# Macaron block on Trainium2: the l part of an item's queries as VectorE's first work in its place of a step

## The chip, the cores and the metric

The kernel runs on one core of a Trainium2 chip, in one launch. The metric is the device time of an execution in microseconds (us).

The core has five engines that run side by side, each through its own list of instructions in order: TensorE (PE in the profile, with its weight loads as PEld), VectorE (DVE), ScalarE (ACT), GpSimd (POOL) and SyncE (SP), which here issues nearly all the DMA transfers. They wait for each other through semaphores. An engine whose next instruction has to wait holds up all that stands behind it in its list.

## The reference, cut to what matters

The input is 4 batches of 4096 rows with 512 columns. Three parts follow each other, each added to the rows:

```python
x = x + 0.5 * ffn(layernorm(x))          # quantised 512x512 product
x = x + attention(layernorm(x))          # 16 heads of 32, 13 neighbours
x = x + 0.5 * ffn(layernorm(x))
```

`ffn` quantises its input in blocks of 32 to a 6-bit grid with a scale per block, multiplies by a weight that is quantised the same way, and adds a bias. `attention` is neighbourhood attention:

```python
qkv = (x @ qkv_w.T + qkv_b).reshape(B, L, 3, HEADS, HEAD_DIM).transpose(2, 0, 3, 1, 4)
q, k, v = (qkv[0] * SCALE, qkv[1], qkv[2])
attn = jnp.einsum('bhld,bhlkd->bhlk', q, kg) + rpb[:, bidx][None]   # kg: 13 keys around each query
attn = jax.nn.softmax(attn, axis=-1)
out = jnp.einsum('bhlk,bhlkd->bhld', attn, vg)
return out.transpose(0, 2, 1, 3).reshape(B, L, C) @ proj_w.T + proj_b
```

## The kernel before

**Numbers in two halves.** Each float32 operand of a large product is held as two float16 parts, h (the value rounded to float16) and l (what the rounding left). `product` (L146) adds three of the four cross products: 12 matmuls of 128x512 into one bank of PSUM. ScalarE writes h, VectorE computes l from the exact value and h. For the queries and keys these are `put_high` (L367) and `put_low` (L371): both read the product in PSUM, and `put_low` reads the h part too.

**Tiles and items.** The rows are cut into 128 tiles of 128 rows. Four tiles make a group. Of each group the attention works on four items, one for each 128 columns (four heads), so there are 128 items as well. A tile goes through `first_half` (the first ffn and the second layernorm), `values`, `project_out` and `second_half`; an item goes through `project_qk`, `softmax` and `attend`. `quantised_norms` makes the quantised input of the two ffns, for two tiles together, and brings it into transposed form by a DMA into `xT`.

**The order is written by hand.** Time is cut into slots. A stage is a generator that ends a piece of work with `yield n, rank`, which puts its next piece n slots later at that rank. Within a slot the pieces run by rising rank:

```python
def run_slot(slot):
    for _, stage in sorted(slots.pop(slot, ()), key=lambda e: e[0]):
        for n, rank in stage:
            begin(slot + n, stage, rank)
            break
```

From L772 on the schedule is manual: each engine gets its instructions in the order in which the pieces run. A new tile and a new item start every 7 slots, so that one round of 7 slots repeats. By its number modulo 7, what each slot holds, in its order of ranks:

- slot 3: the product of an item's queries, `pmqk`; then the product of attention weights and values, `pv`
- slot 4: ScalarE copies `pv` to the ring (L530); VectorE makes the l parts `hlq` and `hln` (L204), and the DMAs that transpose them follow; the product of the item's keys, also `pmqk`; ScalarE writes the queries' h part (L369) and the halo (L382), and the exponentials `sf` (L469)
- slot 5: VectorE writes the l part of the ring (L536); ScalarE the normalised rows `yq` (L233); VectorE the softmax sums `total` (L472 to L474); TensorE the first ffn's product `pmf`; then the second piece of `project_qk`: VectorE the queries' l part (L373) and ScalarE the keys' h part (L369); GpSimd adds biases to two tiles `x` (L564)
- slot 6: VectorE the keys' l part (L373); block maxima `sc` and their reciprocals `r` (L239 to L244); TensorE the values' product `pmv`; GpSimd multiplies `sf` by `total` (L476)
- slot 0: GpSimd scales `yq` by `r` (L246); the second ffn's product `pmf`; scores `ps`
- slot 1: VectorE adds the table to the scores (L458 to L461) and adds the second ffn's product (L275); ScalarE makes the fp8 form `q` (L249) and the attention weights `p` (L480, L481)
- slot 2: the output projection `pmo`; GpSimd scales `q` back (L251)
- slot 3, later ranks: GpSimd makes the l part of `p` (L483), and a DMA transposes it to `pT` (L485)

Every second round some transfers `vs<-vd` (L409) that gather the values for later items are issued as well.

**PSUM.** The products `pmqk`, `pmf`, `pmv` and `pmo` share a pool of three banks, `ps_m` (L93), in the order in which they are begun. A round begins six: queries, keys, `pmf`, `pmv`, the second `pmf`, `pmo`. So `pmv` gets the bank that held the queries' product, and the second `pmf` the one that held the keys'.

Of the kernel before, what the change touches and what calls it, by code (L numbers as in the profile page):

```python
# [64 lines left out]
def macaron_kernel(  # L65
# [80 lines left out]
    def product(pm, lhs, rhs):  # L146

        n = 0
        for a, b in ((0, 1), (1, 0), (0, 0)):
            for c in range(KC):  # L150
                nc.tensor.matmul(  # L151
                    pm, lhs(a, c), rhs(b, c), start=(n == 0), stop=(n == 3 * KC - 1)
                )
                n += 1
# [189 lines left out]
    def item_of(m):  # L344

        g, c = divmod(m, KC)
        return g // NG, g % NG, c

    def project_qk(m):

        b, g, c = item_of(m)
        xg = x2[b * NG + g]
        t = qkp.tile([P, 2, 2, KN + GT], F16, tag="qk", name=f"qk{m}")
        qk[m] = t
        pms = []

        def project(s):
            pm = ps_m.tile([P, GT], F32, tag="mm", name=f"pmqk{s}_{m}")
            pms.append(pm)
            o = (QO, KO)[s] + c * P  # L360
            product(
                pm,
                lambda a, kc: wt[:, a, kc, o : o + P],
                lambda a, kc: xg[:, a, kc].rearrange("p i q -> p (i q)"),
            )

        def put_high(s):  # L367
            bias = qk_b[:, s, c : c + 1]
            nc.scalar.activation(t[:, s, 0, KN:], pms[s], AF.Identity, bias=bias)  # L369

        def put_low(s):  # L371
            bias = qk_b[:, s, c : c + 1]
            nc.vector.scalar_tensor_tensor(  # L373
                t[:, s, 1, KN:], pms[s], bias, t[:, s, 0, KN:], ALU.add, ALU.subtract
            )

        project(0)
        yield 1, 5
        project(1)
        put_high(0)  # L380
        if g > 0:
            nc.scalar.copy(t[:, :, :, :KN], halo[:, c])  # L382
        yield 1, 6
        put_low(0)
        put_high(1)
        if c == KC - 1:
            del x2[b * NG + g]
        yield 1, 0
        put_low(1)
        yield 2, 8  # L390
        if g + 1 < NG:
            nc.scalar.copy(halo[:, c], t[:, :, :, GT:])
# [217 lines left out]
    for m in range(n_items):  # L610
        k = m * STEP
        begin(k + QK, project_qk(m))
        begin(k + SC, softmax(m), 6)
        begin(k + PV, attend(m), 6)
# [297 lines left out]
```

## Time and profile before

| | us |
|---|---|
| median of 3 runs | 2442.0 |
| lowest and highest of them | 2439.76 and 2442.17 |
| the profiled execution's own time | 2436.42 |
| its span, from the first to the last instruction | 2434.6 |
| busy: PE, DVE, POOL, ACT | 2295.3, 2039.3, 1988.3, 1321.0 |

Steps below are worked out on the profiled execution. A line of the timeline gives the start in us from the start of the span, the duration in us, the engine, the line of the code, the operation, the tiles (out<-in), shapes and a count, and in brackets how long the engine sat idle before it and who ended that. Instructions of a kind that follow each other are merged; `x12` is a whole product. Records of matmuls overlap by a little, since their ends are modelled, so products are best compared by their starts.

### The profile page before, as it was taken

Reading aid. Unit: us, or ns where it says so; the run is one execution under the profiler, and the core shown is the slowest. Engines: PE = TensorE matmul, PEld = TensorE weight load, DVE = VectorE, ACT = ScalarE, POOL = GpSimd, SP = SyncE. Lnnn points to the kernel's source line nnn. Section 1 sums busy time; section 2 is a strip of 40 time slices with the busy share of each in tenths; the row PEclk is TensorE's granted clock in tenths of the full one; section 3 lists DMA queues with packets and bytes.
Section 4 is the critical chain, followed back from the end, with each engine's and each line's share of the span. In section 5 each row is a group of like instructions: output and inputs, shape, how many; then the busy total and the mean of one; then the engine's idle time right before and its main releaser. Section 6 shows DMA issues by size and latency. Waiting matters only on the chain.

```text
span 2434.6 us, 82394 instructions
## 1 busy us (share of the span) xinstructions
PE 2295.3 (94%) x35539; PEld 1113.3 (46%) x35539; DVE 2039.3 (84%) x3588; ACT 1321.0 (54%) x2080; POOL 1988.3 (82%) x2012
## 2 busy tenths in 40 slices
PE   0799999999999999999999999999999999999986
PEld 0344444444444444444444444444444444444442
DVE  8788888888888888888888888888888888888776
ACT  4455555555555555555555555555555555555442
POOL 5578888888888888878888888888888888888777
PEclk9899999999999999999999999999999999999998
DMA  5678788787787777778877778777777777777753
GB/s 154 143 145 153 153 161 156 143 152 150 147 159 155 148 147 157 147 144 157 154 146 158 144 152 157 155 148 152 154 140 154 156 157 139 159 148 143 135 110 92
DMA packets 925701, 360.59 MB, mean 148 GB/s; under 512 B 718876, under 2 KB 889752, under 8 KB 925336
## 3 DMA queue, kind: packets, MB, share of 16 engines
q1 hardware_dynamic: 924992, 354.79, 74.4%
q8 instruction: 278, 4.55, 0.8%
q14 instruction: 87, 0.71, 0.1%
q10 hardware_dynamic: 344, 0.53, 0.1%
HBM read 110.15 MB, written 67.29 MB: 73 GB/s over the span
## 4 chain that ended last, share of the span: by engine, by line
PE 67%; DVE 16%; ACT 8%; DMA 5%; issue 3%; POOL 2%; SPq 0%; ACTq 0%; POOLq 0%; DVEq 0%
PE pmf L151 16%; PE pmqk L151 16%; PE pmo L151 13%; PE pmv L151 12%; PE ps L433 6%; DVE total L474 4%; DMA xT<-hlq 4%; DVE total L472 3%; PE pv L503 3%; ACT sf L469 3%; ACT qk L369 2%; DVE qk L373 2%; ACT ring L530 1%; DVE total L473 1%; ACT qk L382 1%
## 5 line engine op out<-in xcount | busy, mean ns | idle before, releaser
L151 PE MATMUL pmf<-wt,xT 128*128 128x512 f16 x3048 | 702.7, 380 | 18.1 <-DMA xT<-hlq 17.7
L151 PE MATMUL pmqk<-x,wt 128*128 128x512 f16 x3072 | 708.6, 380 | 6.0 <-DMA x<-hln 5.3
L151 PEld LDWEIGHTS <-xT 128*128 128x128 f16 x3048 | 296.9, 98 | 386.6 <-DMA xT<-hlq 31.0
L151 PEld LDWEIGHTS <-wt 128*128 128x128 f16 x3072 | 290.2, 98 | 343.3 <-issue 10.2
L246 POOL TENSOR_TENSOR yq<-yq,r 128x1024 f32<-128x1024 f32 (+1 forms) x141 | 246.3, 1747 | 200.5 <-DVE r L244 200.5
L151 PE MATMUL pmv<-wt,x 128*128 128x512 f16 x1536 | 353.5, 380 | 23.5 <-DVE qk L373 14.4
L151 PE MATMUL pmo<-wt,ring 128*128 128x512 f16 x1536 | 356.2, 382 | 2.8 <-issue 2.5
L310 ACT CAST vt<-pmv 128x512 f16<-128x512 f32 x128 | 74.9, 585 | 469.1 <-PE pmv L151 469.1
L564 POOL TENSOR_TENSOR x<-x,half_ffn_b 128x512 f32<-128x512 f32 x256 | 327.3, 1279 | 0.1
L275 DVE SCALAR_TENSOR_TENSOR x<-pmf,coef,x 128x512 f32<-128x512 f32 x256 | 179.7, 702 | 136.9 <-PE pmf L151 136.5
L530 ACT ACTIVATE ring<-pv 128x510 f16<-128x510 f32 (+8 forms) x224 | 82.3, 414 | 368.4 <-PE pv L503 368.4
L180 DVE BATCH_NORM_STATS2 stn<-x 128x6 f32<-128x512 f32 x384 | 265.3, 691 | 9.3 <-DMA x<-in_L_attn_x_dram 0.6
L151 PEld LDWEIGHTS <-x 128*128 128x128 f16 x1536 | 149.9, 98 | 221.6 <-issue 46.4
L251 POOL TENSOR_TENSOR yq<-q,sc 128x1024 f32<-128x1024 fp8e4 (+1 forms) x141 | 246.6, 1749 | 0.0
L249 ACT ACTIVATE q<-yq,nudge 128x1024 fp8e4<-128x1024 f32 (+1 forms) x141 | 150.0, 1064 | 141.6 <-POOL yq L246 133.4
L151 PEld LDWEIGHTS <-ring 128*128 128x128 f16 x1536 | 140.5, 98 | 162.5 <-issue 5.5
L233 ACT ACTIVATE yq<-x,nbq,rsq 128x512 f32<-128x512 f32 x254 | 194.5, 809 | 31.4 <-POOL nbq L192 26.3
L476 POOL TENSOR_TENSOR sf<-sf,total 128x714 f32<-128x714 f32 (+2 forms) x128 | 178.6, 1395 | 37.9 <-DVE total L474 37.4
L483 POOL TENSOR_TENSOR p<-sf,p 128x714 f16<-128x714 f32 (+2 forms) x128 | 192.5, 1504 | 1.2 <-ACT p L480 1.1
L186 POOL TENSOR_SCALAR rsq<-mv 128x2 f32<-128x2 f32 (+1 forms) x141 | 132.0, 936 | 75.0 <-DVE mv L181 72.4
L467 POOL TENSOR_TENSOR sf<-sf,top 128x714 f32<-128x714 f32 (+2 forms) x128 | 180.3, 1409 | 13.8 <-DVE top L465 13.3
L458 DVE TENSOR_TENSOR sf<-ps,table 128x210 f32<-128x210 f32 (+5 forms) x288 | 126.4, 485 | 74.9 <-PE ps L433 74.4
(145 smaller groups left out, 3524.9 us busy)
## 6 DMA issues: line engine op xcount, KB each, us to landing
vs<-vd SPq DMA_DIRECT2D x144, 357.0 KB
x<-in_L_attn_x_dram SPq DMA_DIRECT2D x128, 256.0 KB
vd<-vt SPq DMA_DIRECT2D x128, 256.0 KB
out_dram<-x SPq DMA_DIRECT2D x128, 256.0 KB
vs<-vd SPq DMA_DIRECT2D x24, 378.0 KB
vs<-vd SPq DMA_DIRECT2D x24, 315.0 KB
rows<-in_L_attn_qkv_w_dram SPq DMA_DIRECT2D x12, 256.0 KB
xT<-hlq SPq DMA_TRANSPOSE x141
```

Of the source, the lines that this page charges most:

```text
L151: nc.tensor.matmul(pm, lhs(a, c), rhs(b, c), start=(n == 0), stop=(n == 3 * KC - 1))
L180: nc.vector.bn_stats(st, xs[t])
L233: nc.scalar.activation(y[:, u], xs[t], AF.Identity, bias=nb[:, u : u + 1], scale=rs[:, u : u + 1])
L246: nc.gpsimd.tensor_tensor(yb, yb, bc(r, QB), ALU.mult)
L249: nc.scalar.activation(q8, y, AF.Identity, bias=nudge, saturate=False)
L251: nc.gpsimd.tensor_tensor(yb, q8.rearrange("p u (n q) -> p (u n) q", q=QB), bc(sc, QB), ALU.mult)
L275: nc.vector.scalar_tensor_tensor(xs[t], pm, cf, xs[t], ALU.mult, ALU.add)
L433: nc.tensor.matmul(ps[rows, u, :sides, w * KN : (w + 1) * KN], t[rows, 0, part, q0 : q0 + QR], t[rows, 1, :sides, k0 : k0 + KN], start=par ...
L467: nc.gpsimd.tensor_tensor(s, s, bc(top[:, :n], KN), ALU.subtract)
L476: nc.gpsimd.tensor_tensor(s, s, bc(total[:, :n], KN), ALU.mult)
L483: nc.gpsimd.tensor_tensor(p[:, :n, KN : 2 * KN], s, ph, ALU.subtract)
L564: nc.gpsimd.tensor_tensor(xs[t], xs[t], b, ALU.add)
```

## The change

`project_qk` yields rank -1 in place of 6 ahead of its third piece. The piece holds `put_low(0)`, VectorE's l part of the queries, and `put_high(1)`, ScalarE's h part of the keys. It stays in the same slot (slot 5 modulo 7), where it ran after the rank 0 piece of the ring, the rank 1 piece of the norms, the rank 4 piece of the sums and the rank 5 product `pmf`, and now runs ahead of all of them. No instruction is added, removed or altered, and no DMA is in the piece.

```diff
         if g > 0:
             nc.scalar.copy(t[:, :, :, :KN], halo[:, c])
-        yield 1, 6
+        yield 1, -1
         put_low(0)
         put_high(1)
         if c == KC - 1:
```

## The prediction

> **What bounds the kernel now.** First the page: busy shares, and the row of the product that stands next after the moved piece.
>
> ```profile
> PE 2295.3 (94%) x35539; PEld 1113.3 (46%) x35539; DVE 2039.3 (84%) x3588; ACT 1321.0 (54%) x2080; POOL 1988.3 (82%) x2012
> ...
> L151 PE MATMUL pmv<-wt,x 128*128 128x512 f16 x1536 | 353.5, 380 | 23.5 <-DVE qk L373 14.4
> ```
>
> TensorE leads, and the idle time ahead of `pmv` names DVE's L373, a part of the queries or keys. The 14.4 us are a floor, since records of matmuls overlap and hide the first part of each gap. So next the timeline of PE, once in a round that waits and once in one that doesn't:
>
> ```profile
> 1354.17 2.76 PE L151 MATMUL pmqk<-x,wt 128*128 128x512 f16 x12
> 1356.77 2.75 PE L151 MATMUL pmf<-wt,xT 128*128 128x512 f16 x12
> 1359.70 2.75 PE L151 MATMUL pmv<-wt,x 128*128 128x512 f16 x12 [0.18 <-DVE qk L373]
> 1362.68 2.76 PE L151 MATMUL pmf<-wt,xT 128*128 128x512 f16 x12 [0.23 <-DMA xT<-hlq]
> ```
> ```profile
> 1285.90 2.75 PE L151 MATMUL pmf<-wt,xT 128*128 128x512 f16 x12
> 1288.49 2.75 PE L151 MATMUL pmv<-wt,x 128*128 128x512 f16 x12
> ```
>
> By starts, `pmf` takes 2.59 us when `pmv` can follow (1288.49 - 1285.90) and 2.93 here (1359.70 - 1356.77): 0.34 us lost where the row shows 0.18. Now VectorE, ScalarE and GpSimd in the same round:
>
> ```profile
> 1355.26 0.68 DVE L536 SCALAR_TENSOR_TENSOR ring<-pv,ring 128x510 f16<-128x510 f32 x1
> 1356.54 0.90 DVE L472 TENSOR_REDUCE total<-sf 128x17 f32<-128x714 f32 x1 [0.60 <-ACT sf L469]
> 1357.47 0.27 DVE L473 RECIPROCAL total<-total 128x17 f32<-128x17 f32 x1
> 1357.77 1.22 DVE L474 TENSOR_TENSOR total<-total,p_scale 128x17 f32<-128x17 f32 x1
> 1358.91 1.39 DVE L373 SCALAR_TENSOR_TENSOR qk<-pmqk,qk_b,qk 128x512 f16<-128x512 f32 x2
> 1360.24 1.20 DVE L239 TENSOR_REDUCE sc<-yq 128x32 f32<-128x1024 f32 x1
> ```
> ```profile
> 1354.82 0.68 ACT L369 ACTIVATE qk<-pmqk,qk_b 128x512 f16<-128x512 f32 x1
> 1355.39 0.33 ACT L382 COPY qk<-halo 128x168 f16<-128x168 f16 x1
> 1355.61 0.90 ACT L469 ACTIVATE sf<-sf,coef 128x714 f32<-128x714 f32 x1
> 1356.53 1.52 ACT L233 ACTIVATE yq<-x,nbq,rsq 128x512 f32<-128x512 f32 x2
> 1357.96 0.67 ACT L369 ACTIVATE qk<-pmqk,qk_b 128x512 f16<-128x512 f32 x1
> ```
> ```profile
> 1356.46 1.27 POOL L564 TENSOR_TENSOR x<-x,after_b 128x512 f32<-128x512 f32 x1
> 1357.69 1.27 POOL L564 TENSOR_TENSOR x<-x,half_ffn_b 128x512 f32<-128x512 f32 x1
> 1359.14 1.39 POOL L476 TENSOR_TENSOR sf<-sf,total 128x714 f32<-128x714 f32 x1 [0.18 <-DVE total L474]
> ```
>
> The queries' l part (the first of the two L373) runs from 1358.91 to 1359.65, and `pmv` starts 0.05 us after it. It has been ready to run since its h part ended at 1355.50, but stands behind three sums, of which the first waits 0.60 us for the exponentials and the last, 17 numbers per partition, takes 1.22 us. That last one is not computing all that time:
>
> ```profile
> L474 DVE TENSOR_TENSOR total<-total,p_scale x128: 174/1120/1304, 125.8 to 2374.9; 128x17 f32<-128x17 f32 x80, 128x18 f32<-128x18 f32 x32, 128x16 f32<-128x16 f32 x16
> ```
>
> Its shortest is 0.17 us, its median 1.12: it ends with GpSimd's second bias (1357.69 + 1.27 = 1358.96).
>
> **What the Trainium skill says.** "Trainium Kernel Development and Optimization", section Best Practices: consistent bubbles can mean that SBUF or PSUM ran out. The trace agrees: `pmv` waits for a PSUM bank, in 93 of the 123 rounds that have an item's queries ahead of `pmv`. The same page, section Performance Expectations: matmul busy time is a bad metric, because matmuls are pipelined; here a record is 2.75 us long where the next product starts after 2.59. "SBUF — State Buffer", section Who interferes with whom: a DVE instruction with two SBUF inputs and a GpSimd instruction that reads SBUF exclude each other for a whole instruction, and one with at most one SBUF input is free of that. L474 above agrees; the moved L373, which reads PSUM and one SBUF tile, took 732 to 752 ns in all its 256 executions, so it can be put beside any GpSimd work at its 0.74 us.
>
> **The change, part by part.** Nothing is added or removed, and no DMA and no instruction of GpSimd or TensorE is moved; one DVE and one ACT instruction change places in their lists.
>
> *VectorE's queries.* The l part needs its h part, which ends at 1355.50, while DVE is done with its slot 4 work at 1355.34. So it starts at some 1355.55, ends at 1356.29, and frees the bank 3.3 us earlier than now. `pmv` is wanted at 1356.77 + 2.59 = 1359.36, so the margin is about 3 us. The gain is the whole stall: over the 123 rounds the start of `pmf` to the start of `pmv` exceeds 2.59 us by more than 0.05 in 93, by **33.6 us in sum** (0.3 us in most, over 1.2 in two). After it a round is limited by PE's products alone; rounds without any stall show this already (period 17.49 us with 16 blocks of queries), at the present load of the other engines.
>
> *What it now stands ahead of.* The ring's l part goes from 1355.26 to about 1356.2: its reader, `pmo`, begins at 1366.6, so nothing. The sum L472 starts after it at 1356.84 instead of 1356.54: 0.30 later, because 0.60 of the 0.90 us moved ahead (0.74 and a short wait) fill its wait for the exponentials. L474 then starts at 1358.07, still inside GpSimd's bias, and ends with it at 1358.99 as now. So GpSimd's L476 starts at 1359.14 as now: cost 0, covered by the 0.9 us of L474's blocking. Without this cover L476 would be 0.30 late, before a GpSimd idle time of 1.67 us.
>
> *VectorE's keys and what follows.* At 1358.91 the keys' l part is next in place of the queries', so `sc` and `r` come 0.67 us earlier (1359.57 instead of 1360.24), if `yq` is ready. Where L474 now gets in ahead of the bias (0.18 us; it is under 0.6 in 32 of 128), VectorE will be about 0.3 us later at `sc` instead. Both only shift L246, ahead of which GpSimd idles for `r`.
>
> *ScalarE's keys.* `put_high(1)` now heads ScalarE's slot, and waits for the keys' product: 1354.17 + 2.76 = 1356.93, say 1356.98, to 1357.65. `yq` goes from 1356.53 to 1357.55 and ends at 1359.07, a delay of 1.02 us (0.47 wait, 0.55 to 0.67 work). `sc` wants it at 1359.57: margin 0.5 us, cost 0. Behind it ScalarE has nothing until `vt` at 1362.49. The second `pmf` needs the keys' bank, freed with the keys' l part at 1359.6: it is wanted at 1361.95, so no new stall of that kind.
>
> *What is late next: the DMA of `xT`.* In every fourth round the second `pmf` is just in time for the landing, since the transposition of `hlq` queues on SP behind that of `p`, and that behind `vs`: 1362.68 above has such a wait. The trace shows 13 of these, 6.7 us by starts. If landings kept their time, a `pmv` that comes earlier would wait there again: over all rounds, stall minus slack up to the landing gives back 7.2 us. But the queue's times come from GpSimd's L483, which comes 0.67 us earlier with `r`, as much as PE gains over two rounds. So I take a loss of 2.5 us out of 0 to 7.2; below zero is possible too (the 6.7 us may shrink).
>
> *Sum:* 33.6 - 2.5 = 31 us. The profiled execution would go from 2436.4 to 2405. The median of the runs shown is 5.6 us above the profiled one; the same 31 us off it gives **2411 us**, 1.3% less. About 0.2% (5 us) is what a measurement of this kernel can tell from no change.
>
> **The rivals.**
>
> *A: the stall turns into waits for `xT`.* If the landing keeps its place in every fourth round, 32 in all, and no slack is there, each gives back its 0.33 us: 10.6 us. With L483 no earlier, that is 33.6 - 10.6 = 23 us gained: 2419. For it: SP's transposition of `p` takes 5.38 us in such a round, and DMA is not sped up. Against: many of these rounds have 0.1 to 0.7 us of slack left. Chance 0.14.
>
> *B: slower, through ScalarE's head of the line.* If the keys' product comes so late that `yq` ends after the keys' l part (the point is the 0.5 us margin above), `sc`, `r` and L246, L251, L483 and with them the DMAs slip. If the 1.02 us came through whole, the 32 rounds in which `xT` has no slack would lose 1.02 and the 0.33 won: 43 us against 33.6 gained, 10 us slower: 2452. For it: GpSimd waits 200.5 us for `r`. Against: the margin, and GpSimd's 1.67 us of idle ahead of L246 doesn't help, since that is what would grow. Chance 0.04.
>
> *C: the bank isn't freed by the queries' l part, or the piece isn't first.* Then `pmv` keeps its stall: 2442, 0.03. Against: `pmv` follows the end of the first L373 by 0.05 us in each stalled round, and rank -1 is below all others.
>
> **How the numbers follow.** The forecast 0.79 (2402 to 2416), A 0.14, B 0.04, C 0.03. The low end, 2402, is 33.6 plus all 6.7 us of present `xT` waits; the high end goes beyond A to 2424, where half the stall is left. Faster 0.92, within 0.2% 0.03, slower 0.05.
>
> **What would show it.** In the profile after: `pmv` has no idle time for DVE qk L373, and starts 2.59 us after `pmf`; L373 in the timeline of DVE stands ahead of `ring`, once more after `total`; the wait of `total` for `sf` (75.0 us) falls to near 0; L474's median stays at about 1 us or a little less; the wait of L246 for `r` doesn't grow. Waits of `pmf` for `xT` well over 10 us would show A; `sc` waiting for `yq` would show B; an unchanged stall ahead of `pmv`, C.

## The result, and the profile after

The changed kernel takes 2411.1 us, the median of 4 runs (2401.24 to 2415.96), beside 2442.1 us for the kernel before (2439.76 to 2442.84): a ratio of 0.9871, with a 95% interval of 0.9844 to 0.9898, 31 us less. The profiled execution took 2401.24 us, with a span of 2399.4.

The page of the changed kernel, its busy shares and five of its groups (busy time and mean ns of one, then the idle time ahead of the group and what ended it):

```profile
PE 2278.8 (95%) x35539; PEld 1114.0 (46%) x35539; DVE 2015.3 (84%) x3588; ACT 1327.1 (55%) x2080; POOL 1989.0 (83%) x2012
...
L151 PE MATMUL pmf<-wt,xT 128*128 128x512 f16 x3048 | 703.1, 381 | 17.8 <-DMA xT<-hlq 17.7
...
L151 PE MATMUL pmv<-wt,x 128*128 128x512 f16 x1536 | 353.8, 380 | 5.1 <-DMA x<-hln 5.1
...
L246 POOL TENSOR_TENSOR yq<-yq,r 128x1024 f32<-128x1024 f32 (+1 forms) x141 | 246.2, 1746 | 130.8 <-DVE r L244 130.8
...
L373 DVE SCALAR_TENSOR_TENSOR qk<-pmqk,qk_b,qk 128x512 f16<-128x512 f32 x256 | 190.6, 744 | 53.8 <-ACT qk L369 53.0
...
L369 ACT ACTIVATE qk<-pmqk,qk_b 128x512 f16<-128x512 f32 x256 | 176.1, 688 | 53.2 <-PE pmqk L151 52.1
```

Ahead of `pmv` the name of L373 is gone; the 5.1 us left are one wait in the first rounds. The rows of L373 and L369 are the price of the new order: the queries' l part now waits for its h part (53 us, 5.9 before), and the keys' h part for its product (52.1 us), both off the path of TensorE. For the first and third of these groups, the page of the kernel before has

```profile
L151 PE MATMUL pmf<-wt,xT 128*128 128x512 f16 x3048 | 702.7, 380 | 18.1 <-DMA xT<-hlq 17.7
...
L246 POOL TENSOR_TENSOR yq<-yq,r 128x1024 f32<-128x1024 f32 (+1 forms) x141 | 246.3, 1747 | 200.5 <-DVE r L244 200.5
```

so the waits for `xT` stand where they were by this row, 17.7 us, and GpSimd waits less for `r`.

The timeline of PE over one round:

```profile
1314.60 0.66 PE L503 MATMUL pv<-pT,vs 126*32 126x30 f16 x64
1315.19 2.77 PE L151 MATMUL pmqk<-x,wt 128*128 128x512 f16 x12
1317.80 2.75 PE L151 MATMUL pmf<-wt,xT 128*128 128x512 f16 x12
1320.39 2.75 PE L151 MATMUL pmv<-wt,x 128*128 128x512 f16 x12
1322.98 2.75 PE L151 MATMUL pmf<-wt,xT 128*128 128x512 f16 x12
```

`pmv` follows `pmf` after 1320.39 - 1317.80 = 2.59 us. So it does in all 123 rounds with an item's queries ahead of `pmv`: the excess over 2.59 us, 33.6 us in sum before, is 0.0. The same round on VectorE, then ScalarE, then GpSimd:

```profile
1316.53 0.75 DVE L373 SCALAR_TENSOR_TENSOR qk<-pmqk,qk_b,qk 128x512 f16<-128x512 f32 x1 [0.17 <-ACT qk L369]
1317.20 0.65 DVE L536 SCALAR_TENSOR_TENSOR ring<-pv,ring 128x480 f16<-128x480 f32 x1
1317.77 0.89 DVE L472 TENSOR_REDUCE total<-sf 128x17 f32<-128x714 f32 x1
1318.69 0.27 DVE L473 RECIPROCAL total<-total 128x17 f32<-128x17 f32 x1
1318.99 1.03 DVE L474 TENSOR_TENSOR total<-total,p_scale 128x17 f32<-128x17 f32 x1
1319.94 0.74 DVE L373 SCALAR_TENSOR_TENSOR qk<-pmqk,qk_b,qk 128x512 f16<-128x512 f32 x1
1320.60 1.20 DVE L239 TENSOR_REDUCE sc<-yq 128x32 f32<-128x1024 f32 x1
```
```profile
1318.00 0.69 ACT L369 ACTIVATE qk<-pmqk,qk_b 128x512 f16<-128x512 f32 x1 [0.49 <-PE pmqk L151]
1318.58 1.51 ACT L233 ACTIVATE yq<-x,nbq,rsq 128x512 f32<-128x512 f32 x2
```
```profile
1318.71 1.27 POOL L564 TENSOR_TENSOR x<-x,half_ffn_b 128x512 f32<-128x512 f32 x1
1320.16 1.39 POOL L476 TENSOR_TENSOR sf<-sf,total 128x714 f32<-128x714 f32 x1 [0.18 <-ACT yq L233]
```

L474 still ends with GpSimd's bias: 1318.99 + 1.03 = 1320.02, and 1318.71 + 1.27 = 1319.98. The two L373, one merged record before, now stand at the head of the slot and behind the sums. `yq` ends at 1318.58 + 1.51 = 1320.09, and `sc` starts at 1320.60: the margin on ScalarE's side is 0.51 us. GpSimd's L476, though, is now let go by `yq`: it waits for it in 84 rounds, 19.2 us in sum. With 25.0 us for `total` that makes 44.2, where it waited 37.4 for `total` before.

**Where in the run the time came from.** The starts of `pmv` in PE's timeline, counted from 0, cut the span into stretches that can be compared from kernel to kernel (us):

| | to 10 | 10 to 15 | 15 to 120 | 120 to 127 | after it | span |
|---|---|---|---|---|---|---|
| before | 208.1 | 89.1 | 1892.3 | 120.8 | 124.3 | 2434.6 |
| changed | 205.6 | 87.4 | 1863.7 | 120.7 | 122.1 | 2399.4 |
| changed, second profile | 206.2 | 88.6 | 1865.2 | 119.7 | 125.0 | 2404.8 |
| changed, third profile | 205.6 | 89.0 | 1866.3 | 120.4 | 128.9 | 2410.1 |

In the long middle stretch the first profile is 28.6 us shorter, and the stall ahead of `pmv` was 28.2 us there. The three profiles of the changed kernel differ most in the stretch after the last `pmv`, 6.8 of 10.7 us.

### The profile page after: what moved, and what is told of

It reads as the page before. It is cut to its first block, busy times and chain, and to the rows that moved or that the text cites. A ratio compares the mean times of both kernels' runs of the same rounds, so it can differ in the third digit from the quotient of the medians.

```text
span 2399.4 us, 82333 instructions
## 1 busy us (share of the span) xinstructions
PE 2278.8 (95%) x35539; PEld 1114.0 (46%) x35539; DVE 2015.3 (84%) x3588; ACT 1327.1 (55%) x2080; POOL 1989.0 (83%) x2012
## 3 DMA queue, kind: packets, MB, share of 16 engines
q8 instruction: 278, 4.55, 0.8%
## 4 chain that ended last, share of the span: by engine, by line
PE 89%; DVE 4%; DMA 3%; issue 1%; POOL 1%; ACT 1%; SPq 0%; DVEq 0%; ACTq 0%; POOLq 0%
PE pmqk L151 27%; PE pmf L151 26%; PE pmo L151 14%; PE pmv L151 13%; PE ps L433 6%; PE pv L503 3%; DMA xT<-hlq 2%; DVE hlq L204 0%; DVE fw L749 0%; DMA x<-hln 0%; DVE qk L373 0%; DVE stn L180 0%; POOL x L564 0%; ACT ring L530 0%; DVE whl L779 0%
## 5 line engine op out<-in xcount | busy, mean ns | idle before, releaser
L151 PE MATMUL pmf<-wt,xT 128*128 128x512 f16 x3048 | 703.1, 381 | 17.8 <-DMA xT<-hlq 17.7
L246 POOL TENSOR_TENSOR yq<-yq,r 128x1024 f32<-128x1024 f32 (+1 forms) x141 | 246.2, 1746 | 130.8 <-DVE r L244 130.8
L373 DVE SCALAR_TENSOR_TENSOR qk<-pmqk,qk_b,qk 128x512 f16<-128x512 f32 x256 | 190.6, 744 | 53.8 <-ACT qk L369 53.0
L476 POOL TENSOR_TENSOR sf<-sf,total 128x714 f32<-128x714 f32 (+2 forms) x128 | 178.6, 1395 | 44.2 <-DVE total L474 25.0
L369 ACT ACTIVATE qk<-pmqk,qk_b 128x512 f16<-128x512 f32 x256 | 176.1, 688 | 53.2 <-PE pmqk L151 52.1
```

Source lines behind the costliest of these rows:

```text
L151: nc.tensor.matmul(pm, lhs(a, c), rhs(b, c), start=(n == 0), stop=(n == 3 * KC - 1))
L246: nc.gpsimd.tensor_tensor(yb, yb, bc(r, QB), ALU.mult)
L373: nc.vector.scalar_tensor_tensor(t[:, s, 1, KN:], pms[s], bias, t[:, s, 0, KN:], ALU.add, ALU.subtract)
L476: nc.gpsimd.tensor_tensor(s, s, bc(total[:, :n], KN), ALU.mult)
```

## The experiments

**The theory.** The stall ahead of `pmv` was a wait for the PSUM bank of the queries, whose last reader, the queries' l part, stood on VectorE behind sums that GpSimd's bias blocks. The gain is that stall and nothing else; what is late next is the landing of `xT`. **The rivals:** ScalarE's half of the moved piece has a share in it, or costs something; what counts is to be the first in the slot; the stall and the waits for `xT` are one lost time.

### The two halves of the piece, each alone

VectorE's half alone, with ScalarE's order as before:

```diff
-        put_low(0)
         put_high(1)
...
+        begin(k + QK + 2, one(put, m, "low", 0), -1)
```

> Only VectorE's l part of the queries goes to the head of its slot; ScalarE's h part of the keys stays in its old place. Theory (the gain is the release of the bank for pmv, and that hangs on the queries' l part alone): pmv follows pmf by 2.59 us in every round as in the changed kernel, some 31 us less than before (ratio about 0.987), and ScalarE no longer waits for the keys' product ahead of yq (52 us in the changed kernel, about 1 us before). Rival (ScalarE's half has a share in the gain, since the keys' h part frees the bank of the second pmf): the gain falls clearly below 31 us, to 15 or less.

Measured: 2407.3 us beside 2441.1, ratio 0.9853 (0.9836 to 0.9871). `pmv` follows after 2.59 us in every round. ScalarE's wait for the keys' product and L476's for `yq` are gone from the list of waits, while VectorE's for the queries' h part is 60.7 us. So VectorE's half makes the whole gain; the interval overlaps the changed kernel's, and a difference between the two isn't shown.

ScalarE's half alone:

```diff
         put_low(0)
-        put_high(1)
...
+        begin(k + QK + 2, one(put, m, "high", 1), -1)
```

> Only ScalarE's h part of the keys goes to the head of its slot; VectorE's l part of the queries stays behind the sums. Theory: the stall ahead of pmv stays, about 0.3 us in some 93 rounds, and the time stays within 5 us of before (ratio 0.998 to 1.002). Rival B of the prediction (yq 1.0 us later comes through to sc, r and the transfers of xT): slower by up to 10 us or more, with waits of pmf for xT above the 17.7 us of before. Rival (ScalarE has a share in the gain): 10 us or more faster.

Measured: 2444.8 us beside 2441.1, ratio 1.001 (1.000 to 1.0021). From its page:

```profile
L151 PE MATMUL pmf<-wt,xT 128*128 128x512 f16 x3048 | 703.0, 381 | 19.1 <-DMA xT<-hlq 17.5
...
L151 PE MATMUL pmv<-wt,x 128*128 128x512 f16 x1536 | 353.7, 380 | 22.5 <-DVE qk L373 13.6
```

The stall stays (32.5 us by starts, in 93 rounds), and so do the waits for `xT` by this row (8.7 us by starts in place of 6.7). `yq` waits behind the keys' h part as in the changed kernel, and the time is some 0 to 5 us longer. The price of 43 us that the slower rival of the prediction named isn't there. Whether the small loss comes by `yq` is not shown: with `xT` at 8.7 us, this kernel lies within the 8.0 to 9.7 of the changed kernel's three profiles, given further below.

### Which place in the list is enough

Rank 2 in place of -1: the piece passes the sums, and stays behind the ring and the norms.

```diff
-        yield 1, 6
+        yield 1, 2
         put_low(0)
```

> The piece stands at rank 2: behind the ring's l part and the norms, ahead of the sums. ScalarE's order is that of before. Theory (it is enough to pass the sums and their wait for the exponentials; 3 us of margin ahead of pmv are more than is needed): the queries' l part ends some 0.4 us later than in the changed kernel, still 2.7 us before pmv wants the bank, and the gain is the same 31 us (ratio about 0.987); VectorE's wait for the queries' h part (53 us in the changed kernel) goes to under 10 us, and the sums start some 0.1 us later than before in place of 0.3. Rival (what counts is to be the first in the slot, ahead of the ring): half of the gain or less.

Measured: 2410.4 us, ratio 0.9875 (0.9851 to 0.9899), with no stall ahead of `pmv`. Its list of waits has

```profile
DVE qk L373 <- ACT qk L369: 12.3, 16, 3.4
...
DVE total L472 <- ACT sf L469: 5.0, 17, 1.6
```

(us in total, times, longest). The wait for the h part came out a little above the 10 us expected. To be the first in the slot isn't what counts; to be ahead of the sums is. The 53 us that VectorE waits in the changed kernel and the 12.3 us here make no difference that can be measured.

### The blocked sum alone, without any change of order

```diff
-        nc.vector.tensor_tensor(total[:, :n], total[:, :n], p_scale[:, :n], ALU.mult)
         yield 1, 4
+        nc.scalar.activation(total[:, :n], total[:, :n], AF.Copy, scale=PS)
         nc.gpsimd.tensor_tensor(s, s, bc(total[:, :n], KN), ALU.mult)
```

> The order of before; only the last of the three sums (L474, total times p_scale, median 1.12 us on VectorE) is taken from VectorE and done on ScalarE in slot 6, where ScalarE is idle. Theory (the stall is the time that the queries' l part stands in VectorE's list behind an instruction blocked by GpSimd's bias): the l part starts at once after the reciprocal, 1.1 us earlier in most rounds, and ends at about 1358.5 on the clock of the round shown, 0.8 us before pmv wants the bank; the stall goes without any change of ranks, 28 to 34 us less than before. Rival (the place in the list as such, or ScalarE's new order, makes the gain): no more than 10 us less.

Measured: 2414.8 us, ratio 0.9882 (0.986 to 0.9903), 26 us less, and 2 rounds with 0.5 us of stall in sum. The timeline of VectorE in one of its rounds:

```profile
1323.31 0.90 DVE L472 TENSOR_REDUCE total<-sf 128x17 f32<-128x714 f32 x1 [0.72 <-ACT sf L469]
1324.25 0.27 DVE L473 RECIPROCAL total<-total 128x17 f32<-128x17 f32 x1
1324.43 0.65 DVE L373 SCALAR_TENSOR_TENSOR qk<-pmqk,qk_b,qk 128x512 f16<-128x512 f32 x1
1325.34 0.75 DVE L373 SCALAR_TENSOR_TENSOR qk<-pmqk,qk_b,qk 128x512 f16<-128x512 f32 x1 [0.26 <-ACT qk L369]
```

The order is that of before, with its wait for the exponentials, and the stall is gone. So the stall hung on one multiplication of 17 numbers per partition that stood blocked for a microsecond. The gain is a little under the 28 us expected, though its interval reaches 34: its middle stretch is 1870.5 us, 4 to 7 above the changed kernel's three, without a stall ahead of `pmv`. Most of these few us are stops of TensorE in which it waits for no semaphore, 10.5 us beside 4.9 to 7.2, and 1.7 us of a halved clock; the last table of this section has both.

### What is late next: two tries at the landing of `xT`

The changed kernel as it is, on the chip of the next three:

> The changed kernel as it is, for its time beside the three that follow. Theory (33.6 us of stall go, some 8 us of waits for xT stay): ratio to before about 0.987, 29 to 34 us less. If the gain were an accident of one chip's or one execution's state, the ratio would lie at 0.995 or above.

Measured: 2406.9 us beside 2438.6, ratio 0.9868 (0.985 to 0.9885).

The transposition of p behind those of `hlq` and `hln` on SP:

```diff
+        yield 1, 4
         nc.sync.dma_start_transpose(out=pT[:, :n, :], in_=p[:, :n, :].rearrange("p n k -> p (n k)"))
```

> The changed kernel; only the DMA that transposes p to pT is issued one slot later, behind the transpositions of hlq and hln on SP. Its reader pv comes a round later, so it has time. Theory (what is late next after the stall is the landing of xT, held up on SP by the transposition of p in every fourth round): the waits of the second pmf for xT, 8 us by starts in the profile of the changed kernel, fall below 2 us, and the time by 5 to 8 us under the changed kernel's. Rival (the gathers vs hold up whichever transposition comes first, so the order on SP doesn't matter): waits and time as in the changed kernel within 3 us. Second rival (pT comes too late for pv, or keeps p's buffer from ScalarE): slower than the changed kernel.

Measured: 2430.5 us, ratio 0.9948 (0.9932 to 0.9965): 24 us slower than the changed kernel. From round 11 on, the waits for `xT` are 0.0 by starts, as expected. But its groups show new idle time, and its timeline of PE where some of it lies:

```profile
L151 PE MATMUL pmqk<-x,wt 128*128 128x512 f16 x3072 | 711.9, 381 | 14.9 <-issue 13.1 <-DMA x<-hln 1.9
...
L151 PE MATMUL pmo<-wt,ring 128*128 128x512 f16 x1536 | 360.1, 385 | 13.2 <-issue 13.1
...
L504 PE MATMUL pv<-pT,vs 126*32 126x30 f16 x8768 | 92.5, 180 | 31.6 <-issue 16.6 <-DMA pT<-p 14.9
```
```profile
1419.82 0.42 PE L504 MATMUL pv<-pT,vs 126*32 126x30 f16 x35
1421.49 0.43 PE L504 MATMUL pv<-pT,vs 126*32 126x30 f16 x37 [1.25 <-issue]
```

"issue" is idle time in which the engine waited for nothing that the profile shows. With 2.7 us ahead of `ps`, it adds up to 45.5 us here, and to 13.8 in the changed kernel; the second line is a product that stops in its middle. The expectation failed on the time and held on the mechanism. The second rival had said slower, but not for this reason: the waits of `pv` for `pT` are 14.9 us beside 12.8 in the changed kernel. The granted clock has a share too: from about the end of each of the three longest stops of the rounds in the middle, 2.65 to 3.95 us long, it is 0.5 for 3.4 to 6.8 us.

The same step on the kernel before:

> The kernel before with the same late transposition of p. Theory: the waits for xT (6.7 us by starts) go here too, and the stall ahead of pmv stays (some 0.3 us in some 93 rounds): 4 to 7 us less than before, ratio about 0.998. If the stall ahead of pmv and the waits for xT were one and the same lost time, the gain would be the changed kernel's 30 us or nothing.

Measured: 2449.0 us beside 2438.6, ratio 1.0045 (1.0035 to 1.0056), slower, with waits for `xT` at 0.0 by starts and the stall ahead of `pmv` at 31.4 us. The gain that was expected is lost in the same way, with 31.9 us of "issue" beside 13.8 in the kernel before, but the question is answered: one loss goes without the other.

VectorE's half with the late transposition:

> VectorE's l part of the queries at the head of its slot, ScalarE's h part of the keys in its old place, and the late transposition of p: the best of the parts together. Theory: no stall ahead of pmv, no waits for xT, some 38 to 42 us less than before (ratio about 0.984), within 3 us of the changed kernel with the late transposition. Rival (ScalarE's half has a share of its own): clearly slower than that one.

Measured: 2425.8 us, ratio 0.9939 (0.9921 to 0.9957). It lies 4.7 us under the changed kernel with that step (3 were expected, and the intervals overlap), 13 us under the kernel before and far from the 38 to 42 us expected.

The second gather of a group four slots later, with the transpositions in their old order:

```diff
-        begin(k + 8 * STEP, one(load_stack, b, g, 1), 9)
+        begin(k + 8 * STEP + 4, one(load_stack, b, g, 1), 9)
```

> The changed kernel; only the second gather of a group's values (vs) is issued four slots later, in slot 4 of its round behind the transpositions, as the first one is; the order of the transpositions on SP is the changed kernel's. Theory (the waits of the second pmf for xT in every fourth round come from this gather, which holds up the transposition of p and with it that of hlq): the waits for xT, 8 us by starts in the changed kernel, fall below 2 us, without the new idle time of PE that the late transposition of p brought, and the time is 5 to 8 us under the changed kernel's (ratio to before about 0.984). Rival (any move of DMA work meets TensorE elsewhere, since the queues are shared): time as the changed kernel's or above, with new idle time ahead of pv or inside it.

> The queries' l part alone at the head of its slot, ScalarE in its old order, and the later second gather. Theory: as the changed kernel with the later gather, within 4 us, about 40 us under before. Rival (ScalarE's half matters): apart by more than 6 us.

> The kernel before with the later second gather. Theory (stall ahead of pmv and waits for xT are two separate losses): the stall of about 0.3 us in some 93 rounds stays, the waits for xT (6.7 us by starts) go, 4 to 7 us less than before. Rival (as in the late transposition of p): no gain or a loss, from new idle time of PE elsewhere.

> The changed kernel as it is, on the same chip as the three with the later gather. Theory: ratio to before about 0.987, with no idle time of pmv for the queries' l part and 7 to 9 us of waits for xT by starts.

Measured, all beside 2440.6 us of the kernel before:

| | us | ratio | stall ahead of `pmv`, by starts | waits for `xT`, by starts |
|---|---|---|---|---|
| changed, gather later | 2388.4 | 0.9793 (0.9774 to 0.9812) | 0.0 | 0.0 |
| VectorE's half, gather later | 2389.9 | 0.9795 (0.9777 to 0.9813) | 0.0 | 0.2 |
| before, gather later | 2427.6 | 0.995 (0.9933 to 0.9968) | 31.8 | 0.0 |
| changed | 2407.1 | 0.9866 (0.9846 to 0.9886) | 0.0 | 9.7 |

The first row is the fastest version of this study, 52 us under the kernel before. VectorE's half alone is 1.4 us from it, as expected. The waits for `xT` come from this gather, since they go when it is moved. But the gains are larger than expected, 19 us under the changed kernel for 5 to 8, and 13 us under the kernel before for 4 to 7, and the stretches say that the reason given is not where they come from:

| | to 10 | 10 to 15 | 15 to 120 | 120 to 127 | after it |
|---|---|---|---|---|---|
| changed, gather later | 198.5 | 84.4 | 1864.0 | 119.1 | 119.0 |
| before, gather later | 201.0 | 87.5 | 1896.3 | 120.2 | 120.4 |

Where the waits for `xT` were, in the middle, 1864.0 us is no less than the first profile's 1863.7 and 1 to 2 less than the other two. There stops inside `pmo` have taken their place, in the page's groups and in PE's timeline:

```profile
L151 PE MATMUL pmf<-wt,xT 128*128 128x512 f16 x3048 | 703.3, 381 | 12.5 <-DMA xT<-hlq 12.5
...
L151 PE MATMUL pmo<-wt,ring 128*128 128x512 f16 x1536 | 357.4, 382 | 7.8 <-issue 7.4
```
```profile
1725.23 1.90 PE L151 MATMUL pmo<-wt,ring 128*128 128x512 f16 x8
1729.97 1.70 PE L151 MATMUL pmo<-wt,ring 128*128 128x512 f16 x4 [2.84 <-issue]
```

(the 12.5 us of `xT` are waits at the two ends of the run). Right behind this stop, and behind one of 2.29 us at 1121.5, the granted clock is 0.5 for 3.41 us. The middle stretch can be taken apart. "Half clock" is an estimate: half of the time in which the granted clock was 0.5.

| from 15 to 120, us | length | stall ahead of `pmv` | waits for `xT` | "issue" | half clock | what is left |
|---|---|---|---|---|---|---|
| before | 1892.3 | 28.2 | 5.9 | 7.8 | 0.0 | 1850.4 |
| changed | 1863.7 | 0.0 | 7.9 | 4.9 | 0.0 | 1850.9 |
| changed, second profile | 1865.2 | 0.0 | 8.8 | 5.0 | 0.0 | 1851.4 |
| changed, third profile | 1866.3 | 0.0 | 7.8 | 7.2 | 0.0 | 1851.3 |
| blocked sum on ScalarE | 1870.5 | 0.0 | 5.9 | 10.5 | 1.7 | 1852.4 |
| changed, late transposition | 1889.1 | 0.0 | 0.0 | 31.4 | 6.8 | 1850.9 |
| before, late transposition | 1896.3 | 24.1 | 0.0 | 20.1 | 0.0 | 1852.1 |
| changed, gather later | 1864.0 | 0.0 | 0.0 | 9.5 | 3.4 | 1851.1 |
| before, gather later | 1896.3 | 27.2 | 0.0 | 14.9 | 3.4 | 1850.9 |

With these four losses off, kernels whose stretches differ by 33 us come within 2 us of each other. So the waits for `xT` were worth their 8 us, and "issue" and the clock took them back.

The gain lies in the first 15 rounds, 10 to 12 us, and after the last `pmv`, 3 to 10 us. In the first 15 rounds, `pmqk`'s wait for `x<-hln`, "issue" and half clock make 11.2 us in place of 19.2 to 21.5 in the changed kernel's three profiles; after the last `pmv`, "issue" and half clock make 6.8 in place of 11.7 to 19.2. These sums are of the size of the gain, and upper estimates where TensorE had nothing to do at half clock. Why a later gather shortens them stays open. The stall ahead of `pmv` and this gain add up, as far as the intervals can tell: 13 us for the gather alone and 31 to 34 for the order in the runs above make 44 to 47, beside 52 (46 to 55) for both.

## Why the prediction was right, point by point

The order of events in a round, as us after the start of `pv`, from the round that the prediction used, its working, and the round shown above (whose `pv` is 0.03 us shorter):

| | before | predicted | after |
|---|---|---|---|
| queries' l part starts | 5.37 | 2.01 | 1.93 |
| ring's l part | 1.72 | 2.7 | 2.60 |
| L472 | 3.00 | 3.30 | 3.17 |
| L474 ends | 5.45 | 5.45 | 5.42 |
| `yq` starts | 2.99 | 4.01 | 3.98 |
| `sc` starts | 6.70 | 6.03 | 6.00 |
| L476 starts | 5.60 | 5.60 | 5.56 |
| `pmv` starts | 6.16 | 5.82 | 5.79 |

*The stall:* predicted to go whole, 33.6 us; it went whole. It was also the right cause: the order of VectorE's half, or the removal of the blocked sum, takes it away, and ScalarE's half doesn't.

*The costs put at nothing:* they were nothing. The sums start later and end when GpSimd lets them; L474's blocking took up the delay, and its median fell from 1.12 us to 0.81:

```profile
L474 DVE TENSOR_TENSOR total<-total,p_scale x128: 175/811/1086, 125.5 to 2339.6; 128x17 f32<-128x17 f32 x80, 128x18 f32<-128x18 f32 x32, 128x16 f32<-128x16 f32 x16
```

The wait of `total` for the exponentials fell from 75.0 us to 1.6. One cost was not on the list, the waits of L476 for `yq`; VectorE's half alone is without them, and no difference in time is shown. What "SBUF — State Buffer" of the Trainium skill states in its section Who interferes with whom carried this step: a VectorE instruction with two SBUF inputs and a GpSimd instruction that reads SBUF contend for a shared port pair, under an exclusive lock. The trace agrees: in the profile before, 105 of the 128 L474 took over 0.3 us, and each of them ends within 0.06 us of the end of a GpSimd instruction. The run with the sum on ScalarE confirms that this was blocking and not work: there the rest of VectorE's order is untouched, and its busy time falls from 2039.3 to 1932.6 us for 128 multiplications whose shortest was 0.17 us.

*`sc` and `r`:* 0.70 us earlier in this round, where 0.67 was predicted; GpSimd's wait for `r` fell from 200.5 to 130.8 us.

*The waits for `xT`:* a loss of 2.5 us was taken, out of 0 to 7.2. By starts they went from 6.7 us to 8.0, 8.7 and 9.7 in the three profiles, a loss of 1.3 to 3.0. Rival A's 10.6 us is not there. The reason that the prediction gave against it fits: GpSimd's L483, which sets the queue's times, starts 8.40 us behind `pmv` in place of 8.75 (medians of the middle rounds), so it came forward by more than `pmv` did.

*The sum:* 31 us predicted, 31.0 between the medians. That the two agree so closely is luck: the interval reaches from 25 to 38 us. The mechanism doesn't rest on it. The profiled execution gained 35.2, 4 more than the sum: 28.6 in the middle, and 2.5, 1.7, 0.1 and 2.2 in the other stretches of the table. In the middle that is the stall of 28.2, less 2.0 for `xT`, and 2.9 us less of "issue", which the prediction did not have. The ends vary by more than the rest from profile to profile.

*Rival B* failed on its own margin: 0.5 us predicted between `yq` and `sc`, 0.51 measured. *Rival C* is excluded by the first half alone.

## What to carry to other kernels

When the busiest engine waits for a bank, look for the bank's last reader and for what stands ahead of it in its engine's list; a sum over a few numbers can be the longest thing there, if another engine's lock holds it. Measure such a stall by the starts of the products, not by the idle time that the row shows (33.6 us against 14.4). And after a gain, test what is late next by itself: the waits for `xT` were real and could be removed twice, yet stops of TensorE in other places took the gain back both times, and what the second try won came from the two ends of the run.

## What the runs showed of the hardware that was not expected

TensorE can stop in the middle of a product, with no semaphore to wait for. In the changed kernel with the late transposition, between 300 and 2200 us, there are 20 such stretches above 0.35 us, 31.1 us in sum, at 236 starts of a block (see below); in the changed kernel there are 5 at 232. "Runtime: NRT & Kernel Launch" of the Trainium skill, section Instruction fetch mechanics, states that each engine's sequencer fetches its instructions by its own DMA queue in blocks of 16 KiB, at a cost that is mostly hidden. The trace agrees on the size: 278 packets and 4.55 MB on the queue q8, whose kind is "instruction", 16.4 KB each. TensorE's own list has 71203 entries in that kernel, so one packet stands for 256 of them.

Counted along this list in steps of 256, all 143 stretches of this kind in the fourteen profiles of this study begin at one and the same place of a step, entry 194 or 195. Each ends 1.2 to 2.0 us after the packet of the same number on q8 has ended, and in none of these profiles, stop or no stop, does TensorE start on a block sooner than 1.2 us after its packet (all between 300 and 2200 us). So in these stretches TensorE waited for its own instructions. That is how moving one DMA by one slot costs 24 us without any new wait on a semaphore that fits. Whether the kernel's own transfers made those packets late is not shown: no run changed the packets alone.

Such a stop can cost more than its length: behind some of the longer ones the granted clock was 0.5 for 3.41 us or twice that, as the experiments above show. It does not follow each of them: in the kernel before, a stop of 2.49 us at 1043.6 has a full clock behind it.
